# Adding gathers, and chunks prepared by VectorE's 32x32 transposes

## The chip, the cores and the metric

The kernel runs on one core of a Trainium2 chip. The metric is the device time of one execution in microseconds (us). Its engines work side by side, each on a stream of instructions in a fixed order: TensorE (PE, matmuls and transposes by matmul), VectorE (DVE), ScalarE (ACT), GpSimd (POOL), and SyncE (SP), which issues most of the DMAs. Instructions wait for each other through semaphores.

## What is computed

The input `x` is (4, 32, 128, 128) in float32. Layer 0 is an attention between channels; layer 1 reads its result as tokens of 128 values, adds a linear attention, and then a mixture of eight experts, of which each token takes the best two.

```python
# layer 0: 2x2 space to depth gives 128 "channels" of 4096 positions in each image
q = xs.reshape(B, C*R*R, hw)
energy = einsum('bci,bcj->bij', q, q)
d = sqrt(diagonal(energy))
attn = softmax(energy / (d[:, :, None] * d[:, None, :]), axis=-1)
x = gamma * einsum('bcj,bij->bci', q, attn) + xs           # and depth back to space
# layer 1: tokens t of D = 128
t = t + linear_attention(layernorm(t))                      # 8 heads
top_p, top_i = top_k(softmax(layernorm(t) @ router_w + router_b), 2)
out = t + sum_k top_p[k] * (layernorm(t) @ expert_w[top_i[k]] + expert_b[top_i[k]])
```

As the einsums have it, `energy` runs over the 4096 positions i, j and sums over the 128 channels, so it is 4096x4096 for each of the four images.

## The kernel before

**Layer 0.** The 4096 positions of an image are cut into eight chunks of 512. `attend(b)` goes through row chunks i = 0..7 and, as `energy` is symmetric, only through column blocks up to i. For each block TensorE makes `pe` (line 550) from the normalised chunk `qn`; ScalarE takes the exponential and its sum into `pr` (553); TensorE multiplies `pr` into the output `po` (439). The block's mirror image is had by transposing: VectorE turns 32x32 pieces (`F`, 368), SyncE sends them through memory (472, 487) so that the pieces change places, and TensorE multiplies them into `pg` (374), which VectorE adds to the output `o` (384). ScalarE sums them up once more (`junk`, 379).

**Preparation.** `prep(b, kc)` makes two chunks at a time ready, sixteen times in all, four for each image. SyncE loads rows `xx` with tokens on the partitions (278); TensorE transposes them eight times into `ptq` (312); VectorE copies the result to `qT` (301), squares it (323), and sums (324); GpSimd raises the sums to -1/2 (`rn`, 163); VectorE multiplies (`qs`, 337); TensorE transposes eight times more into `ptn` (345); ScalarE copies to `qn` (343). In image 0 the first preparation stands before everything, and `keep_running` gives TensorE spare transposes while it waits. The rows that layer 1 needs again (`T`) are loaded by `input_rows`.

**Layer 1.** `close_rows` (673) divides the output by its sums, adds the input (`df`, 703; `T`, 725), takes the mean and variance for the layer norm (728), with the power `rsa` on GpSimd (163), and normalises into `xn` on ScalarE (638). `matrix`, `attention_rows` and a router follow, with a second norm whose power is `rsf`. For images 0 to 2, `sorted_experts` then works in two halves of 16 groups of 128 rows: it scatters each row twice into a buffer `xs` sorted by expert (indirect DMAs from GpSimd's queue, 989), loads tiles of that buffer (1015), multiplies each by its expert (1058, 1051), copies the result (1034) and stores it in `ys`, gathers the two rows of each token from `ys` (`yb`, 1116) and adds them with their weight to `acc` on VectorE (1085), which had been fetched from memory. For image 3, whose layer 1 has no attention beside it, all eight experts are computed densely (`py`, 1200), and nothing is sorted.

**Order.** PE, DVE, ACT and SP are in an order written out by hand: instructions stand in each engine's queue as the program emits them. The main loop (1325 to 1368) runs through the steps of `attend`, and after each lets other generators go one step. Those in `timed` have a begin and an end in per cent of the image and a count of steps; those in `steady`, the layer-1 stream of the image before, go a step each ten units of a clock of 1568 units per image. GpSimd's powers and gathers are kept in their program order by `pinned`. Scatters and gathers also wait for the newest exponential (`exps`), so that no more of them run than the steps have. `hold` gives out a bank of PSUM and its eviction. The layer-1 work of image b runs beside the attention of image b+1.

Of the kernel before, what the change touches and what calls it, by code (L numbers as in the profile page):

```python
# [22 lines left out]
def kernel(  # L23
# [94 lines left out]
    NT = 2 * HR + E - 1  # L118
    rank_below = const.tile([P, P], F32, tag="below", name="rank_below")
# [5 lines left out]
    xs = [dram.tile([NT * P, D], F32, tag=f"xs{h}", name=f"xs_{h}", bufs=1) for h in range(2)]  # L125
# [9 lines left out]
    def setup_sorting():  # L135
# [14 lines left out]
        rows = x.rearrange("b c h w -> (b c h) w")  # L150
# [130 lines left out]
    def prep(b, kc, st):  # L281

        if b == 0:
            if kc == 0:
                st["all"] = big1.tile([P, 4, 8, HW2, 2], F32, tag="T", name="xx_0")
            xx = st["all"][:, kc]
        else:
            xx = xin.tile([P, 8, HW2, 2], F32, tag="xx", name=f"xx_{b}_{kc}")
        first = b == 0 and kc == 0
        load_tokens(  # L290
            xx.rearrange("p k w r -> p k (w r)"), b, 8 * kc, 8, (nc.sync, nc.scalar if first else nc.sync)
        )
# [3 lines left out]
        yield  # L296
        yield
        yield from idle(2 if b else 1)

        def load_half(g, pt):  # L300
            nc.vector.tensor_copy(
                qT[:, :, 2 * g : 2 * g + 2, :].rearrange("p s j (r c) -> p (j r) s c", c=64),
                pt.rearrange("p (m s c) -> p m s c", s=2, c=64),
            )

        for g in range(2):
            yield
            pt, done = hold(f"ptq_{b}_{kc}_{g}", partial(load_half, g))
            for jj in range(2):
                for r2 in range(2):  # L310
                    k = 4 * g + 2 * jj
                    nc.tensor.transpose(  # L312
                        pt[:, ts(2 * jj + r2, P)], xx[:, k : k + 2, :, r2].rearrange("p k w -> p (k w)"), ident
                    )
            yield
            done()
        yield
# [3 lines left out]
        for s in range(2):  # L321
            sq = work.tile([P, NJ, P], F32, tag="qs", name=f"sq_{b}_{kc}_{s}", bufs=2)
            nc.vector.tensor_tensor(sq, qT[:, s], qT[:, s], ALU.mult)
            nc.vector.tensor_reduce(ss[:, ts(s, NJ)], sq, AX.X, ALU.add)  # L324
            if first:
                pow_neg_half(rn[:, ts(s, NJ), 0], ss[:, ts(s, NJ)])
            elif s == 1:
                pow_neg_half(rn[:, :, 0], ss)
            yield
            yield  # L330
        yield from idle(1)
        if first:
            keep_running(22, ps_g, "pg")
# [5 lines left out]
        for s, qs in enumerate(scaled):  # L339
            yield  # L340
            qn = npool.tile([P, CH], F32, tag="qn", name=f"qn_{b}_{2 * kc + s}")
            st.setdefault("qn", {})[2 * kc + s] = qn
            pt, done = hold(f"ptn_{b}_{kc}_{s}", lambda p, qn=qn: nc.scalar.activation(qn, p, AF.Copy))  # L343
            for j in range(NJ):
                nc.tensor.transpose(pt[:, ts(j, P)], qs[:, j, :], ident)
            yield
            done()
        yield
        yield
# [19 lines left out]

    def transposed_share(b, st, i, jc, G):  # L370

        pg = ps_g.tile([P, CH], F32, tag="pg", name=f"pg_{b}_{i}_{jc}")
        for ib in range(NJ):
# [8 lines left out]
            if ib == NJ - 1:  # L382
                o = st["o"][jc].rearrange("p (j a c) -> p a j c", a=4, c=S)
                nc.vector.tensor_tensor(o, o, pg.rearrange("p (a j c) -> p a j c", a=4, c=S), ALU.add)  # L384
                st["got"][jc] += 1
            yield "done" if ib == NJ - 1 else None

    def diagonal_share(b, st, i, G):
# [3 lines left out]
        for step in ((3,), (2, 1)):  # L392
# [9 lines left out]
            if step == (2, 1):  # L402
                o = st["o"][i].rearrange("p (j a c) -> p a j c", a=4, c=S)[:, :, :3]
                nc.vector.tensor_tensor(
                    o, o, pg[:, : 3 * P].rearrange("p (a j c) -> p a j c", a=4, c=S), ALU.add
                )
                st["got"][i] += 1
# [8 lines left out]
    def attend(b, st):  # L416
# [11 lines left out]
        for i in range(NCH):  # L428
# [5 lines left out]
            def values(w, blk, lo, hi, i=i, row=row):  # L434
# [7 lines left out]
                if row["left"] == 0:  # L442
                    o = opool.tile([P, CH], F32, tag="o", name=f"o_{b}_{i}")
                    nc.scalar.activation(o, row["po"], AF.Copy)  # L444
                    st["o"].append(o)
# [63 lines left out]
            def back(w, j, jc, i=i):  # L509
# [7 lines left out]
                if j == NJ - 1:  # L517
                    nc.vector.tensor_tensor(st["o"][jc], st["o"][jc], row["back"], ALU.add)
# [68 lines left out]
    def input_rows(b, st):  # L587
        st["T"] = T = big1.tile([P, KT, D], F32, tag="T", name=f"T_{b}")
        nk = 4 if b == 0 else 8
        for k in range(0, KT, nk):  # L590
            load_tokens(T[:, k : k + nk, :], b, k, nk)
            yield
            yield
            yield from idle(1)

    def layer1(b, st):
# [3 lines left out]
        xn = big1.tile([P, KT, D], F32, tag="xn", name=f"xn_{b}")  # L600
# [5 lines left out]
        place = stat.tile([P, 2, KT], U32, tag="place", name=f"place_{b}", bufs=1)  # L606
# [29 lines left out]
        def normalise(rows, rs, nb):  # L636
            for k in rows:
                nc.scalar.activation(xn[:, k, :], T[:, k, :], AF.Identity, scale=rs[:, k, :], bias=nb[:, k, :])  # L638

        def transpose_rows(g):  # L640
            pt, done = hold(f"ptx_{b}_{g}", partial(keep_rows, g))
            for j in range(4):
                nc.tensor.transpose(pt[:, ts(j, P)], xn[:, 4 * g + j, :], ident)
# [15 lines left out]
        def gram_rows(rows):  # L659
# [9 lines left out]
            for k in rows:  # L669
                nc.tensor.matmul(p[:, :D], xn[:, k, :], xn[:, k, :], start=(k == rows[0]), stop=(k == rows[-1]))  # L670
            return done

        def close_rows(kc):
# [23 lines left out]
            def divide(pb):  # L697
                for s in range(2):
                    own = slice(s * 64, s * 64 + 64)
                    o = st["o"][2 * kc + s]  # L700
                    for r2 in range(2):
                        rows = slice(r2 * 64, r2 * 64 + 64)
                        nc.vector.tensor_tensor(  # L703
                            df[own, :, :, r2],
                            o[rows].rearrange("p (k w) -> p k w", w=HW2),
                            pb[own].rearrange("p (k w) -> p k w", w=HW2),
# [29 lines left out]
            if late_rows:  # L736
                for j in range(k + 4, k + 8):
                    nc.vector.tensor_scalar(
                        xn[:, j, :], T[:, j, :], rsa[:, j, :], nba[:, j, :], ALU.mult, ALU.add
# [122 lines left out]
        def transpose_tokens(g, alloc=psum_t):  # L862
# [3 lines left out]
                lambda p: nc.scalar.activation(xn[:, ts(g, 4), :], p.rearrange("p (j t) -> p j t", t=P), AF.Copy),  # L866
                alloc,
            )
            for j in range(4):
                nc.tensor.transpose(pt[:, ts(j, P)], xn[:, 4 * g + j, :], ident)  # L870
# [43 lines left out]
        def sorted_experts(h):  # L914
# [72 lines left out]
            for n in range(2 * HR):  # L987
                k, i = r0 + n // 2, n % 2
                inst = nc.gpsimd.indirect_dma_start(xs[h], offset(place[:, i, k : k + 1]), xn[:, k, :], None)  # L989
# [11 lines left out]
                if h == 1 and n in (7, 15):  # L1001
                    yield from idle(2)
# [11 lines left out]
            def load(g, n):  # L1014
                inst = nc.sync.dma_start(bufs[g % 4][:, :n], rows_of(xs[h], g, n))
# [3 lines left out]
            def products(turned, applied):  # L1019


                def leave(p):
                    if turned:
                        g, n = turned
                        nc.scalar.activation(  # L1025
                            bufs[4 + g % 2][:, :n], p[:, : n * P].rearrange("p (j t) -> p j t", t=P), AF.Copy
                        )
                    if applied:
                        g, n = applied
                        if g % 4 < 2:  # L1030
                            result = bufs[6 + g % 2]
                        else:
                            result = work.tile([P, 2, D], F32, tag="grp", name=f"result_{b}_{h}_{g}", bufs=2)
                        nc.vector.tensor_copy(  # L1034
                            result[:, :n], p[:, 2 * P : 2 * P + n * D].rearrange("p (j c) -> p j c", c=D)
# [4 lines left out]
                if applied:  # L1040
# [9 lines left out]
                    for j in range(n):  # L1050
                        nc.tensor.matmul(  # L1051
                            p[:, 2 * P + j * D : 2 * P + j * D + D], bufs[4 + g % 2][:, j, :],
                            weights[:, bass.ds(begins[2 * (g % 2) + j], D)], start=True, stop=True,
                        )
                if turned:
                    g, n = turned
                    for j in range(n):
                        nc.tensor.transpose(p[:, ts(j, P)], bufs[g % 4][:, j, :], ident)  # L1058
                return done

            done = None
# [18 lines left out]
            accs, yb = {}, {}  # L1080

            def combine(n):
                k, i = r0 + n // 2, n % 2
                a = accs[k // 4]
                nc.vector.scalar_tensor_tensor(
                    a[:, k % 4, :], yb[k // 4][:, i, k % 4, :], weight[:, i, k, :], a[:, k % 4, :], ALU.mult, ALU.add
                )
                if k % 4 == 3 and i == 1:
                    after_steps.append((now[0] + 2, partial(put, k // 4)))

            def fetch(g):
                nc.scalar.dma_start(accs[g], t2[:, ts(g, 4)])
# [7 lines left out]
            dst_out = tokens(out, b)  # L1100
            after_steps = []
            now = [0]

            def due():
                now[0] += 1
                for at, f in [q for q in after_steps if q[0] <= now[0]]:
                    f()
                after_steps[:] = [q for q in after_steps if q[0] > now[0]]

            for n in range(2 * HR):  # L1110
                k, i = r0 + n // 2, n % 2
                if k % 4 == 0 and i == 0:
                    accs[k // 4] = work.tile([P, 4, D], F32, tag="acc", name=f"acc_{b}_{k // 4}", bufs=3)
                    after_steps.append((now[0] + 1, partial(fetch, k // 4)))
                    yb[k // 4] = work.tile([P, 2, 4, D], F32, tag="wide", name=f"yb_{b}_{k // 4}")
                inst = nc.gpsimd.indirect_dma_start(  # L1116
                    yb[k // 4][:, i, k % 4, :], None, ys, offset(place[:, i, k : k + 1])
                )
                wait_for(pinned(inst).ins, exps, "not more of these at a time than steps have")
# [288 lines left out]
```

## Time and profile before

| | before |
|---|---|
| median of 3 runs, us | 1698.8 |
| lowest and highest | 1698.34, 1700.94 |
| profiled execution, us | 1704.26 |
| its span, us | 1702.5 |
| mean TensorE clock granted | 0.993 |
| HBM read, written, MB | 153.85, 175.24 |

The profiled execution has its own time, 5.5 us above the median; durations below are from it. A group's line in the profile gives the code line, the engine and its operation, the tiles written and read with their form, how often, then busy time in us with the mean of one in ns, and last the idle time of the engine just before, with what ended it. These are the groups that the change touches:

```profile
L312 PE MATMUL ptq<-ident,xx 128*128 128x128 f32 x128 | 21.0, 290 | 9.3 <-DMA xx<-in_x_dram 9.3
L345 PE MATMUL ptn<-ident,qs 128*128 128x128 f32 x128 | 20.3, 283 | 6.8 <-issue 6.1 <-DVE qs L337 0.6
L301 DVE COPY qT<-ptq 128x512 f32<-128x512 f32 x32 | 21.7, 679 | 31.8 <-PE ptq L312 25.7 <-PE pe L550 6.1
L337 DVE TENSOR_TENSOR qs<-qT,rn 128x512 f32<-128x512 f32 x32 | 20.6, 681 | 1.5 <-POOL rn L163 1.5
L1085 DVE SCALAR_TENSOR_TENSOR acc<-yb,weight,acc 128x128 f32<-128x128 f32 x192 | 65.7, 343 | 4.0 <-DMA acc<-t 0.5
L1116 POOL DMA_INDIRECT yb<-ys,place x192 | 185.3, 965 | 246.7 <-ACT pr L553 67.9 <-DMA xn<-xs 63.2 <-issue 44.0
```

Read the first: TensorE made 128 transposes of `xx` into `ptq`, the records of one lasted 290 ns on average, and TensorE stood idle for 9.3 us before some of them, until a load of `xx` had landed. Records of neighbouring matmuls overlap, so busy times on PE add up to more than the engine's time. A piece of the chain of waits has a start in us, a length, and the line of the instruction that the end of the run depended on there. A line of a wait list names who waited, for whom, and the total in us, how many times, and the longest.

### The profile page before, as it was taken

How to read it: one execution, taken by the hardware profiler on the slowest of the kernel's cores; microseconds unless marked ns; L12 is line 12 of the kernel's file. 1: busy time of each engine (PE TensorE's matmuls, PEld its weight loads, DVE VectorE, ACT ScalarE, POOL GpSimd, SP SyncE). 2: the span in 40 equal slices, each digit the busy share in tenths (PEclk: the TensorE clock that was granted, in tenths of full speed). 3: DMA queues.
4: the chain of work that ended last, by engine and by line, in shares of the span. 5: the costliest groups of instructions: out<-in, count | busy, mean ns of one | idle time of the engine just before them, and what ended most of it. 6: DMA issues, size and time to landing. Idle time of an engine off the chain costs nothing.

```text
span 1702.5 us, 21925 instructions
## 1 busy us (share of the span) xinstructions
PE 1651.5 (97%) x5458; PEld 876.1 (51%) x5458; DVE 936.7 (55%) x2443; ACT 926.0 (54%) x2893; POOL 511.0 (30%) x553
## 2 busy tenths in 40 slices
PE   8999999999999999999999999999999999998888
PEld 5444444455554555445554455545555455554643
DVE  4433334467485345478478334556748533454787
ACT  3555445466575555446565555545656455544476
POOL 1000000011026425451015642543102642446166
PEclk9999999999999999999999999999999999999999
DMA  4554756754458777875457777886445876876001
GB/s 135 168 177 157 204 173 219 242 190 162 149 173 266 229 239 243 255 225 161 136 179 235 228 248 240 236 258 194 165 141 167 264 228 216 254 243 193 7 12 39
DMA packets 227053, 325.51 MB, mean 191 GB/s; under 512 B 31472, under 2 KB 155504, under 8 KB 212592
## 3 DMA queue, kind: packets, MB, share of 16 engines
q1 hardware_dynamic: 206416, 285.15, 52.3%
q0 software_dynamic: 12288, 25.19, 5.1%
q10 hardware_dynamic: 8224, 13.77, 2.8%
q8 instruction: 46, 0.75, 0.2%
q14 instruction: 79, 0.65, 0.1%
HBM read 153.85 MB, written 175.24 MB: 193 GB/s over the span
## 4 chain that ended last, share of the span: by engine, by line
PE 79%; DVE 8%; DMA 4%; ACT 3%; issue 2%; SPq 2%; POOL 1%; another core or an unknown queue 0%; ACTq 0%; DVEq 0%; POOLq 0%
PE po L439 22%; PE pe L550 22%; PE pg L374 19%; PE pys L1051 3%; PE py L1200 3%; PE pg L395 2%; PE pys L1058 1%; PE pat L796 1%; ACT xn L638 1%; SPq L487 1%; DMA F<-blocks 1%; DVE df L703 1%; PE pgram L670 1%; PE ptq L312 1%; DMA blocks<-F 1%
## 5 line engine op out<-in xcount | busy, mean ns | idle before, releaser
L553 ACT ACTIVATE pr<-pe 128x512 f32<-128x512 f32 (+1 forms) x576 | 322.4, 560 | 552.0 <-PE pe L550 420.6
L439 PE MATMUL po<-pr,qT 128*128 128x512 f32 (+3 forms) x1152 | 551.9, 561 | 6.3 <-ACT o L444 5.6
L550 PE MATMUL pe<-qn,qn 128*128 128x512 f32 x896 | 462.5, 598 | 5.2 <-ACT pr L553 4.9
L374 PE MATMUL pg<-F,qT 128*128 128x512 f32 x880 | 451.1, 594 | 1.3 <-DMA F<-blocks 1.3
L368 DVE STREAM_TRANSPOSE F<-pr 128x512 f32<-128x512 f32 x440 | 305.8, 702 | 165.8 <-ACT pr L553 144.2
L439 PEld LDWEIGHTS po<-pr,qT 128*128 128x128 f32 x1152 | 216.0, 191 | 254.1 <-issue 223.7
L379 ACT ACTIVATE junk<-F 128x512 bf16<-128x512 f32 x440 | 272.9, 620 | 1.4 <-DMA F<-blocks 1.4
L374 PEld LDWEIGHTS pg<-F,qT 128*128 128x128 f32 x880 | 167.5, 191 | 197.2 <-issue 182.4
L1116 POOL DMA_INDIRECT yb<-ys,place x192 | 185.3, 965 | 246.7 <-ACT pr L553 67.9
L989 POOL DMA_INDIRECT xs<-xn,place x192 | 185.8, 968 | 163.0 <-ACT pr L553 86.7
L550 PEld LDWEIGHTS pe<-qn,qn 128*128 128x128 f32 x896 | 154.3, 192 | 114.7 <-issue 98.2
L384 DVE TENSOR_TENSOR o<-o,pg 128x512 f32<-128x512 f32 x110 | 75.4, 685 | 189.5 <-PE pg L374 156.2
L163 POOL TENSOR_TENSOR rn<-ss,neg_half 128x8 f32<-128x8 f32 (+1 forms) x17 | 26.9, 1584 | 332.6 <-DVE ss L324 332.5
L553 ACT ACTIVATION_READ_ACCUMULATOR pr<-pe 128x1 f32 x576 | 112.1, 195 | 0.0
L1025 ACT ACTIVATE xn<-pys 128x256 f32<-128x256 f32 x120 | 45.3, 378 | 109.8 <-PE pys L1058 87.5
L163 POOL TENSOR_TENSOR rsf<-dm_f,neg_half 128x8 f32<-128x8 f32 (+1 forms) x15 | 26.2, 1744 | 233.7 <-DVE sv_f L630 233.7
L1051 PEld LDWEIGHTS pys<-ew_sb,xn 128*128 128x128 f32 x468 | 69.6, 191 | 46.6 <-issue 43.8
L550 PE MATMUL pe<-qn 128*128 128x512 f32 (+3 forms) x256 | 90.4, 435 | 0.7 <-ACT qn L343 0.7
L379 ACT ACTIVATION_READ_ACCUMULATOR junk<-F 128x1 f32 x440 | 84.4, 192 | 0.0
L163 POOL TENSOR_TENSOR rsa<-dm_a,neg_half 128x8 f32<-128x8 f32 x16 | 26.5, 1654 | 186.5 <-DVE sv_a L630 186.2
L1034 DVE COPY xn<-pys 128x256 f32<-128x256 f32 x60 | 25.4, 424 | 89.2 <-ACT xn L1025 68.7
L1034 DVE COPY result<-pys 128x256 f32<-128x256 f32 (+1 forms) x60 | 24.6, 410 | 87.1 <-ACT xn L1025 57.8
(212 smaller groups left out, 1655.4 us busy)
## 6 DMA issues: line engine op xcount, KB each, us to landing
blocks<-F SPq DMA_DIRECT2D x110, 1024.0 KB
F<-blocks SPq DMA_DIRECT2D x220, 192.0 KB
F<-blocks SPq DMA_DIRECT2D x220, 128.0 KB
xn<-xs SPq DMA_DIRECT2D x114, 128.0 KB
F<-blocks SPq DMA_DIRECT2D x220, 64.0 KB
below<-F SPq DMA_DIRECT2D x31, 384.0 KB
out_dram<-acc SPq DMA_DIRECT2D x128, 64.0 KB
xx<-in_x_dram SPq DMA_DIRECT2D x62, 128.0 KB
```

Of the source, the lines that this page charges most:

```text
L163: pinned(nc.gpsimd.tensor_tensor(dst, src, neg_half.to_broadcast(list(src.shape)), ALU.pow))
L368: f()
L374: nc.tensor.matmul(pg.rearrange("p (a f) -> p a f", a=4), st["qT"][i][:, ib, :], G[:, :, ib], start=(ib == 0), stop=(ib == NJ - 1),)
L379: nc.scalar.activation(junk, G[:, :, ib], AF.Copy, accum_out=st["sums"][:, NJ * i + ib, jc : jc + 1])
L384: nc.vector.tensor_tensor(o, o, pg.rearrange("p (a j c) -> p a j c", a=4, c=S), ALU.add)
L439: nc.tensor.matmul(row["po"][:, lo:hi], qT[blk // NJ][:, blk % NJ, :], w, start=start, stop=(row["left"] == 0))
L550: nc.tensor.matmul(pe[:, c0:], qn[jc][:, ts(j, P)], qn[i][:, c0:], start=True, stop=True)
L553: nc.scalar.activation(pr[:, c0:], pe[:, c0:], AF.Exp, accum_out=sums[:, t, i : i + 1]).ins
L989: inst = nc.gpsimd.indirect_dma_start(xs[h], offset(place[:, i, k : k + 1]), xn[:, k, :], None)
L1051: nc.tensor.matmul(p[:, 2 * P + j * D : 2 * P + j * D + D], bufs[4 + g % 2][:, j, :], weights[:, bass.ds(begins[2 * (g % 2) + j], D)], sta ...
L1116: inst = nc.gpsimd.indirect_dma_start(yb[k // 4][:, i, k % 4, :], None, ys, offset(place[:, i, k : k + 1]))
L1200: nc.tensor.matmul(bank, xn[:, k, :], ew_sb[:, 4 * h : 4 * h + 4, :], start=True, stop=True)
```

## The change

The change has four parts.

1. *Preparation.* A chunk's transposed rows `qT` are made by VectorE. Rows are loaded by quarters (`load_quarters`, `xa`, with channels on the partitions in groups of 32), and four 32x32-block transposes write `qT` in place of eight TensorE transposes and two copies. `qn` is made from the rows `xx` (token order), which VectorE multiplies with a bank of PSUM that holds `rn` spread out: two copies (`wide`), four TensorE transposes (`pnorm`) and four products (`scale`) stand in place of two products, eight transposes and two ScalarE copies. The columns of a chunk come in another order for that, so some views of `o` and `df` change. The first preparation (`prep_first`) keeps the eight transposes into `ptn`, and has 40 spare transposes rather than 22.
2. *Loads and placement.* For image 0 the rows `T` are loaded by the preparations, and `input_rows` is used for images 1 to 3 alone. For images 1 to 3 a preparation loads both `xa` and `xx`. Preparations have 16 steps rather than 12 or 13, over longer stretches of the image.
3. *Rows with their weight.* A row of `xs` has 132 values, of which the last four repeat the row's weight; GpSimd writes them into `xn` before each half of the scatters. The result of an expert is multiplied by that weight as it leaves PSUM, so `ys` holds weighted rows. Loads have six buffers rather than four.
4. *Adding gathers.* `acc` is fetched first, and the gathers add to it in the DMA itself (`compute_op`). VectorE's 192 combines and the tile `yb` go. The second four gathers of a group add to the same rows as the first four and wait for them. Gathers come one to two generator steps (images 0 and 1), or two with a pause after each four (image 2). Scatters have more pauses.

```diff
+    def load_quarters(b, kc, queues=(nc.sync, nc.sync)):
+        xa = xin.tile([P, 2, 2, 2, HW2, 2], F32, tag="xx", name=f"xa_{b}_{kc}")
+        halves = x[b].rearrange("c (s g) w -> c s (g w)", s=2)
+        for a in (0, 2, 1, 3):
+            first_row = 16 * kc + 4 * a
+            queues[a // 2].dma_start(
+                xa[ts(a, S)].rearrange("p s k r w e -> p s (k r w e)"),
+                halves[:, :, first_row * W : (first_row + 4) * W],
+            )
+        return xa
+    def turn_quarters(s, xa, qT):
+        for k in range(2):
+            nc.vector.transpose(
+                qT[:, s, 2 * k : 2 * k + 2, :].rearrange("p h (e r c) -> p r (h e) c", e=2, r=2),
+                xa[:, s, k].rearrange("p r (h t) e -> p (r h) e t", h=2),
+            )
...
     def prep(b, kc, st):
-        for g in range(2):
-            pt, done = hold(f"ptq_{b}_{kc}_{g}", partial(load_half, g))
-            for jj in range(2):
-                for r2 in range(2):
-                    k = 4 * g + 2 * jj
-                    nc.tensor.transpose(
-                        pt[:, ts(2 * jj + r2, P)], xx[:, k : k + 2, :, r2].rearrange("p k w -> p (k w)"), ident
-                    )
+        for s in range(2):
+            turn_quarters(s, xa, qT)
+            yield
+        if b > 0:
+            xx = xin.tile([P, 8, HW2, 2], F32, tag="xx", name=f"xx_{b}_{kc}")
+            load_tokens(xx.rearrange("p k w r -> p k (w r)"), b, 8 * kc, 8)
...
+        def scale(s, spread, view):
+            qn = channels(b, kc, s, st)
+            own = slice(s * 64, s * 64 + 64)
+            for r2 in range(2):
+                nc.vector.tensor_tensor(
+                    qn[ts(r2, 64)].rearrange("p (j a t) -> p a j t", a=4, t=S),
+                    xx[own].rearrange("p (a k) (h t) r -> p r a (k h) t", a=4, h=2)[:, r2],
+                    view(spread[own]), ALU.mult,
+                )
...
+        wide = work.tile([P, NJ, 2, 64], F32, tag="qs", name=f"wide_{b}_{kc}", bufs=2)
+        for s in range(2):
+            nc.vector.tensor_copy(wide[:, :, s], rn[:, ts(s, NJ)].to_broadcast([P, NJ, 64]))
         yield
+        bank, done = hold(f"pnorm_{b}_{kc}", scale_all)
+        for j in range(NJ):
+            nc.tensor.transpose(bank[:, ts(j, P)], wide[:, j].rearrange("p s c -> p (s c)"), ident)
...
             for n in range(2 * HR):
-                k, i = r0 + n // 2, n % 2
-                inst = nc.gpsimd.indirect_dma_start(xs[h], offset(place[:, i, k : k + 1]), xn[:, k, :], None)
+                i, k = n // HR, r0 + n % HR
+                if n % HR == 0:
+                    pinned(
+                        nc.gpsimd.tensor_copy(xn[:, half, D:], weight[:, i, half, :].to_broadcast([P, HR, DW - D]))
+                    )
...
-                        nc.vector.tensor_copy(
-                            result[:, :n], p[:, 2 * P : 2 * P + n * D].rearrange("p (j c) -> p j c", c=D)
+                        result = keep["results"][:, g % 4]
+                        nc.vector.tensor_tensor(
+                            result[:, :n], p[:, 2 * P : 2 * P + n * D].rearrange("p (j c) -> p j c", c=D),
+                            bufs[g % 6][:, :n, D : D + 1].to_broadcast([P, n, D]), ALU.mult,
                         )
...
+            rate = 1 if b < B - 2 else 2
+            fetch(groups[0])
+            yield from idle(2)
+            for g in groups:
+                for n in range(8):
+                    i, k = n // 4, 4 * g + n % 4
+                    inst = nc.gpsimd.indirect_dma_start(
+                        accs[g][:, n % 4, :], None, ys, offset(place[:, i, k : k + 1]), compute_op=ALU.add
+                    )
+                    wait_for(pinned(inst).ins, exps, "not more of these at a time than steps have")
+                    if (n + 1) % rate == 0:
+                        yield
+                        yield
+                    if rate == 2 and n % 4 == 3:
+                        yield from idle(1)
+                    if n == 3 and g != groups[0]:
+                        put(g - 1)
+                    if n == 3 and g != groups[-1]:
+                        fetch(g + 1)
...
-            for kc, begin, end in ((1, 0, 5), (2, 6, 20), (3, 25, 45)):
-                timed.append((prep(0, kc, states[0]), begin, end, 12))
+            for kc, begin, end in ((2, 6, 22), (3, 25, 48)):
+                timed.append((prep(0, kc, states[0]), begin, end, 16))
...
-            timed.append((prep(b + 1, 0, nxt), 65, 82, 13))
-            timed.append((prep(b + 1, 1, nxt), 87, 99, 13))
-        begin, end, count = (52, 94, 17) if b == 0 else (36, 47, 9)
-        timed.append((input_rows(b, states[b]), begin, end, count))
+            timed.append((prep(b + 1, 0, nxt), 52, 78, 16))
+            timed.append((prep(b + 1, 1, nxt), 80, 99, 16))
+        if b > 0:
+            timed.append((input_rows(b, states[b]), 36, 47, 9))
...
-            timed.append((prep(b + 1, 2, nxt), 2, 20, 13))
-            timed.append((prep(b + 1, 3, nxt), 30, 50, 13))
+            timed.append((prep(b + 1, 2, nxt), 1, 22, 16))
+            timed.append((prep(b + 1, 3, nxt), 28, 52, 16))
```

## The prediction

> **What bounds the kernel now.** I read the page's busy times first, then the chain of waits in order of time in a quiet stretch, then TensorE's wait list, and then the chain again wherever that list had an entry.
>
> ```profile
> PE 1651.5 (97%) x5458; PEld 876.1 (51%) x5458; DVE 936.7 (55%) x2443; ACT 926.0 (54%) x2893; POOL 511.0 (30%) x553
> ...
> 642.02 0.86 PE pg L374 x2
> 642.87 0.47 PE ptq L312 x4
> 643.34 0.45 PE pys L1051 x4
> ...
> 656.97 0.86 PE pe L550 x2
> ```
>
> TensorE is busy 97% of the span, and in the quiet stretch one matmul group begins where the last ends: a group taken out of it shortens the kernel by its pace on the chain. That pace is 0.43 us for a 512-wide matmul and 0.47 us for four transposes; the group table's mean of 290 ns for one transpose has the overlap of pipelined matmuls in it and must not be multiplied.
>
> ```profile
> PE ptq L312 <- DMA xx<-in_x_dram: 9.3, 3, 5.7
> PE ptn L345 <- issue: 6.1, 2, 3.1
> PE po L439 <- ACT o L444: 5.6, 13, 2.0
> ...
> 711.96 3.12 DMA acc<-t
> ...
> 717.00 1.37 SPq L278
> 718.41 4.54 DMA xx<-in_x_dram
> ...
> 723.41 0.72 PE ptq L312 x4
> 724.13 1.52 PE pe L550 x2
> ...
> 746.47 1.36 issue
> 747.84 0.91 PE ptn L345 x4
> 748.75 1.71 PE pe L550 x2
> ```
>
> The wait list totals what TensorE lost and for whom. The two largest entries belong to the chunk preparation. In images 1 and 2 the same thing happens twice: at 711 and 1118 us SyncE stands behind a fetch of `acc`, so rows arrive late for `ptq`; at 747 and 1149 us `ptn` waits while VectorE works off a queue of combines, gated differences and transposes. After such a gap a pair of `pe` takes 1.71 us where 0.86 is usual. At the four places TensorE waits 2.06, 3.07, 1.52 and 3.07 us, and the slow matmuls after them lose 2.9, 1.9, 0.5 and 3.2 us (their pieces minus their usual pace): 18.2 us together.
>
> **The Trainium skill.** "TensorE: Matmul & The Clock Gate", Part 1, says that the clock halves after an idle window of some 3.4 us and returns after about as long at work. The trace agrees in kind, 0.86 to 1.71 us, though 3.07 us of idling were enough. "DMA: Bandwidth & Descriptors", in the part on SWDGE and HWDGE, says that adding during a transfer belongs to GpSimd's DMAs; its rules for kernel authors say that an adding DMA reads its destination and writes it later with nothing held between, so a second add to the same rows must wait for the first. The trace of before has no adding DMA. "VectorE: DVE Perf Modes", The three transpose paths, says that VectorE turns 32x32 blocks only; hence the new loads by quarters and the changed column order. Its one trace form here is `F` (L368, 702 ns for 128x512).
>
> **The change, part by part.** Sums are against the profiled execution, 1704.3 us (span 1702.5), which stands 5.5 us above the median of 1698.8; I carry the difference over to the median.
>
> *Preparation on TensorE.* A preparation of two chunks now has 8 `ptq` and 8 `ptn`; after, four transposes into one bank. Four `ptn` take 0.44 us on the chain. 2x0.47 + 2x0.44 - 0.44 = 1.38 us, times 15 preparations (the first is separate): -20.7 us, all on the bounding engine.
>
> *Preparation elsewhere.* VectorE loses two `qT` copies (679 ns) and two `qs` products (681) and gains four 128x256 transposes (0.42 us each, estimated between the 283 ns of a 128x128 and 702 of a 128x512), two 128x256 copies (367, as L694) and four 64x512 products from PSUM (687, as L703): +2.4 us each, +37 us in all. The 192 combines go: -65.7. The products of result and weight take the place of copies (424 ns) at about their price. VectorE thus falls by some 29 us from 936.7, which costs and gains nothing directly. ScalarE loses 2x0.59 us x15 = 18 us. The output evictions that become strided and the reordered gated difference I take at their old price; bounds -0.1 to +0.2 us each, some 150 of them, beside TensorE's work.
>
> *Loads.* Images 1 to 3 load each chunk pair twice, by quarters and by rows: 48 more issues of 128 KB, image 0 16 fewer 64 KB ones, so SyncE issues 32 more at 0.45 us = 14 us over 1700; 6.3 MB on 325.5. Every step is stretched over 16 stream steps rather than 13, so a load stands 5 steps (some 24 us) ahead of its transposes where it took 4.5 to 5.8 us. A SyncE wait as at 711 us then no longer reaches TensorE. If this cover went, each chunk pair would cost the 5 us of before.
>
> *First chunk.* Before: rows land at 5.5, eight `ptq` to 7.7, copies, first `pe` at 13.64. After: two transposes (0.84) in place of `ptq` and a copy (2.7), -2 us. The 40 spare matmuls at 0.19 us (22 took 4.21) make 7.6 us, need no loaded row and end by about 10, before `ptn`.
>
> *Stalls of 18.2 us.* The `ptq` ones (7.0) lose their consumer. The `ptn` ones (11.2) come from VectorE's backlog, which loses its combines but gets 2.4 us more of preparation. Bounds 0 and -18; I take -12, as `pnorm` waits only for VectorE's small copies, but its products must still be made before the chunk's turn, at i=4, 21% into the image: 19.4% is where the plan puts them, some 6 us of cover.
>
> *Adding gathers in the middle.* POOL's instruction count stays at 192 gathers and 192 scatters of 0.96 us, plus twelve small copies. In images 0 and 1 the gathers are spread one to two stream steps (5 us), 64 over 320 us where they took 160; a fourth-next gather waits for the first to land, 20 us later, hidden for any credible landing. What queues behind a waiting gather on POOL are the powers `rn`, `rsa`, `rsf`, and behind these VectorE and ScalarE's `xn`: 0 to +8 us, I take +2. Rows of 528 rather than 512 bytes in `xs`: 3% on 25 MB, nothing.
>
> *The tail.* Here POOL is on the chain.
>
> ```profile
> L1116 POOL DMA_INDIRECT yb<-ys,place x10: 943/948/1036, 1560.9 to 1572.4; - x10
> ...
> 1593.91 1.64 POOL rsa L163
> ...
> 1605.12 0.18 DVE dm_a L627
> 1605.78 1.64 POOL rsa L163
> ...
> 1607.73 0.50 ACT xn L638
> 1608.27 2.07 PE pgram L670 x16
> ```
>
> Before, ten gathers of image 2 started from 1560.9 to 1572.4, 1.26 us apart, and none stood between the `rsa` of 1593.9 and that of 1605.8. After, the slower pace leaves 20 of image 2's gathers in POOL's order between these two. From the end of the earlier one, 1595.8 less the 2.2 us of combines that leave the chain there, 20x1.26 = 25.2 us: `rsa` begins at 1619 rather than 1605.8, +13 us on the path to the end. TensorE idles over 10 us meanwhile and starts slowly: +3 us, as after the gaps above. Bounds: 0 if most of the 20 are issued earlier in POOL's idle time; and if an add takes longer to land than four issues (5.04 us), each of three second halves of a group waits the difference. I take a landing of 5 us, an estimate from the 2.75 to 3.1 us of `acc<-t` and a read of the destination besides: +16 in all.
>
> Sum: -20.7 - 2 - 12 + 2 + 16 = -16.7, so 1687.6 by the profiled execution and about 1682 against the median.
>
> **Rivals.**
> (a) *Slower than before: slow adds in the tail.* Should an add take 14 us to land, the three waits add 3x9 = 27 to the sum of -16.7: +10, so 1709. It decides from a landing of 5.04 + 16.7/3 = 10.6 us on. For it: nothing in before shows such an add, and POOL's next power stands in line behind all of them. Against it: ten plain gathers were issued back to back with semaphores reused eight apart, so a plain one lands within some 10 us.
> (b) *No tail cost.* The 20 gathers go out in gaps, or the last rows are late for other reasons: -20.7 - 2 - 12 - 2 = -37, with some stall left 1665. For it: POOL sat idle 9.96 us before the `rsa` of 1605.8. Against it: order on an engine is fixed, and their predecessors wait for exps.
> (c) *The stalls stay or move.* `qn` is now made by VectorE, with no ScalarE help; when it is late at i=4, a 3 us gap and the slow clock cost 5 us per image, and the 12 us saved are paid back: 1694. For it: 6 us of cover only, and VectorE's slices reach 8 tenths there.
> (d) *The change doesn't do what it says*: transposes leave TensorE by the instruction order; no chance given.
>
> **How the numbers follow.** Main case 1682 (1674 to 1690), 0.47; (b) 1665, 0.18; (c) 1694, 0.16; (a) 1709, 0.19, into which I put a power on POOL that is late by more than its +8 as well. Leaving out the ends of (a) and (b): 1658 to 1706. A measurement of this kernel can tell about 0.2%, 3.4 us, from no change: bounds 1695.4 and 1702.2. Main and (b) are faster, of (c) two fifths (0.06): 0.71. Of the rest of (c) 0.09 falls within and a little above: slower 0.20.
>
> **What would show it.** Right: no `ptq` and TensorE busy some 21 us less; first `pe` near 11.7; no TensorE gap over 2 us in the stretches of 700 to 760 and 1115 to 1160; VectorE near 908; the last `rsa` near 1590 with a string of gathers before it. Wrong: a gather whose semaphore wait lasts over 5 us in mid-image; `pe` waiting for `qn` at i=4; powers on POOL late behind gathers; TensorE's clock row under 9 in a middle slice.

## The result, and the profile after

The changed kernel takes 1704.2 us (median of 7 runs, 1701.5 to 1706.0) beside 1698.3 for the kernel before: a ratio of 1.0037, interval 1.0025 to 1.0048. The forecast was 1682. A repeat beside other runs (e12 below) gave 1703.2 and 1.0073 (1.006 to 1.0086). So the change makes the kernel slower by 0.4 to 0.7%; the profiled spans, 1702.4 after and 1702.5 before, hide this, because the first trace of before was an execution 5.5 us above its median. A second trace of before (e4) has a span of 1696.0; it is used for comparisons below where it is named. The kernel before took 1698 to 1700 us beside the first runs and 1690 to 1692 beside e5 to e12, so times are compared beside each other's before, and a lead read between traces of different sets of runs can be off by several us.

The page of the changed kernel first: busy times, the granted clock by slices, the software DMA queue (packets, MB, share), and the group of the gathers.

```profile
PE 1629.5 (96%) x5288; PEld 858.7 (50%) x5288; DVE 910.2 (53%) x2343; ACT 913.3 (54%) x2863; POOL 630.5 (37%) x565
...
PEclk9999999999999999999999999999999999999699
...
q0 software_dynamic: 33792, 25.58, 8.5%
...
L1162 POOL DMA_INDIRECT acc<-ys,place x192 | 301.4, 1570 | 300.1 <-ACT pr L610 171.2
```

TensorE is busy 22 us less and VectorE 26 us less, as the change meant. GpSimd is busy 120 us more, and 116 of these are in the gathers: 1570 ns each where 965 were. The software queue moves the same 25 MB in 33792 packets where it had 12288. In one slice near the end the clock is at 6 tenths.

TensorE's wait list after (who waited for whom; us in total, times, longest):

```profile
PE pgram L726 <- ACT xn L694: 34.4, 4, 29.6
PE pnorm L397 <- DVE F L419: 5.8, 3, 2.0
PE pe L607 <- ACT pr L610: 5.0, 7, 1.9
...
PE pnorm L397 <- DVE wide L388: 2.5, 1, 2.5
```

In images 1 and 2 neither the wait of before for `xx` nor that of `ptn` for VectorE is left. One wait of 29.6 us has come, and smaller ones for `pnorm`. The chain of waits, in order of time, shows where the large one ends:

```profile
1563.13 0.04 POOL rsa L164
...
1565.58 0.30 POOL acc L1162
...
1599.62 1.54 POOL acc L1162
1601.16 0.30 issue
1601.46 1.54 POOL acc L1162
1603.00 1.72 POOL rsa L164
...
1605.03 0.50 ACT xn L694
...
1605.58 3.79 PE pgram L726 x16
...
1609.74 2.73 PE pgv L837 x6
```

Between the two `rsa` stand GpSimd's adding gathers without a break. The last `rsa`, and with it `xn`, `pgram` and all that ends the kernel, waits for the last of them. Before, the same `rsa` began at 1605.78 right after its operand; now it begins at 1602.45 (the timeline's own start of it), although the attention ended 30.7 us earlier than in that trace (1566.7 against 1597.4). `pgram` takes 3.79 us where it took 2.07.

How far each kernel had come, in us: ScalarE's copy of each image's eighth row chunk to `o` (called the end of the image below), the start of the last `rsa`, and the span. "Before" is the second trace.

| | before (e4) | adds only (e6) | prep only (e5) | changed |
|---|---|---|---|---|
| image 0 | 365.1 | 366.2 | 358.9 | 358.3 |
| image 1 | 769.5 | 762.3 | 760.1 | 753.6 |
| image 2 | 1173.3 | 1160.4 | 1159.9 | 1152.0 |
| image 3 | 1592.0 | 1571.5 | 1573.4 | 1566.7 |
| last `rsa` | 1600.4 | 1607.3 | 1581.8 | 1602.5 |
| span | 1696.0 | 1707.0 | 1678.4 | 1702.4 |

By the end of the attention the changed kernel is 25.3 us ahead; at the last `rsa` it is 2.1 us behind.

### The profile page after: what moved, and what is told of

Its sections match the earlier page's. It is cut to its first block, busy times and chain, and to the rows that moved or that the text cites. A ratio compares the mean times of both kernels' runs of the same rounds, so it can differ in the third digit from the quotient of the medians.

```text
span 1702.4 us, 21468 instructions
## 1 busy us (share of the span) xinstructions
PE 1629.5 (96%) x5288; PEld 858.7 (50%) x5288; DVE 910.2 (53%) x2343; ACT 913.3 (54%) x2863; POOL 630.5 (37%) x565
## 3 DMA queue, kind: packets, MB, share of 16 engines
q0 software_dynamic: 33792, 25.58, 8.5%
## 4 chain that ended last, share of the span: by engine, by line
PE 77%; DVE 10%; DMA 4%; POOL 3%; ACT 2%; issue 2%; SPq 1%; DVEq 0%; ACTq 0%; POOLq 0%
PE po L495 22%; PE pe L607 21%; PE pg L431 19%; PE pys L1111 3%; PE py L1247 2%; POOL acc L1162 2%; PE pgram L726 2%; PE pg L451 2%; DVE F L419 2%; PE pys L1118 1%; PE pat L852 1%; DVE df L759 1%; DMA blocks<-F 1%; SPq L543 1%; DMA F<-blocks 1%
## 5 line engine op out<-in xcount | busy, mean ns | idle before, releaser
L1162 POOL DMA_INDIRECT acc<-ys,place x192 | 301.4, 1570 | 300.1 <-ACT pr L610 171.2
L1093 DVE TENSOR_TENSOR results<-pys,xn 128x256 f32<-128x256 f32 x120 | 49.8, 415 | 183.8 <-ACT xn L1087 146.3
L694 ACT ACTIVATE xn<-T,nba,rsa 128x128 f32<-128x128 f32 x120 | 49.2, 483 | 44.6 <-POOL nba L688 44.6
L726 PE MATMUL pgram<-xn 128*128 128x128 f32 x256 | 38.7, 294 | 34.7 <-ACT xn L694 34.4
L1111 PE MATMUL pys<-ew_sb,xn 128*128 x468 | 71.6, 274 | 0.0
```

The lines of the kernel that those rows point to most:

```text
L726: nc.tensor.matmul(p[:, :D], xn[:, k, :D], xn[:, k, :D], start=(k == rows[0]), stop=(k == rows[-1]))
L1093: nc.vector.tensor_tensor(result[:, :n], p[:, 2 * P : 2 * P + n * D].rearrange("p (j c) -> p j c", c=D), bufs[g % 6][:, :n, D : D + 1].to_ ...
L1111: nc.tensor.matmul(p[:, 2 * P + j * D : 2 * P + j * D + D], bufs[6 + g % 2][:, j, :D], weights[:, bass.ds(begins[2 * (g % 2) + j], D)], st ...
L1162: inst = nc.gpsimd.indirect_dma_start(accs[g][:, n % 4, :], None, ys, offset(place[:, i, k : k + 1]), compute_op=ALU.add)
```

## The experiments

**e4: before again.** No edit.

> The kernel before itself, for a second trace. If TensorE's four stalls beside the preparation of images 1 and 2 (18 us in the first trace) belong to the kernel, they are there again, of the same length; if they belong to that one execution, which was 5.5 us above the median, some are missing and the span is near 1697.

The ratio to before was 1.0012 (0.9997 to 1.0028). The span was 1696.0 and the stalls were all there:

```profile
PE ptq L312 <- DMA xx<-in_x_dram: 10.9, 3, 5.7
PE ptn L345 <- issue: 6.1, 2, 3.1
```

They belong to the kernel (5.7 of the first line is the start). At the four places the timeline has 2.62, 3.07, 2.51 and 3.07 us, against 2.06, 3.07, 1.52 and 3.07 in the first trace. The difference between the two traces lies elsewhere, some 3 us of it in image 3 (from the end of image 2 to that of image 3 it is 418.7 us here, 421.7 in the first trace), and was not traced further.

**e5 and e6: each half alone.** e5 has the new preparation, loads, column order and placement, with plain gathers and VectorE's combines; e6 has the rows with their weight and the adding gathers, with the old preparation.

> The kernel before with the new preparation, loads, column order and placement alone; gathers plain, combined on VectorE, in the old order. TensorE's removed transposes (20.7) and the first chunk (2) give 22.7; the stalls of before give 0 to 12 more: 1664 to 1676 by theory A, in which the preparation is good and the gathers lose it. If the preparation itself gains little (its VectorE work turns up in waits), 1685 to 1698.

> The kernel before with rows that carry their weight and adding gathers alone; preparation as before. Theory A: 20 gathers at 1.84 us stand between the last two rsa: 36.9 us from 1593.6, so the last rsa begins near 1630 in place of 1605.8, +25, and +3 for the clock; less what stalls go with the combines (0 to 11): 1715 to 1727. If adding gathers cost nothing on the path to the end, 1687 to 1698.

e5: 1677.4 beside 1692.4, ratio 0.9909 (0.9892 to 0.9926). e6: 1708.4, ratio 1.0095 (1.0078 to 1.0111). So the adding gathers alone make the kernel slower and the preparation alone makes it faster. e6's list shows both halves of its effect:

```profile
PE pgram L671 <- ACT xn L639: 30.8, 5, 29.6
PE ptq L313 <- DMA xx<-in_x_dram: 5.8, 1, 5.8
```

The last wait is as long as in the changed kernel, and of the stalls of images 1 and 2 none is left (5.8 is the start). The table says the same: without one transpose removed, e6 is 20.5 us ahead of before at the end of image 3, and 6.9 behind at the last `rsa`. With that lead e6 stayed below the 1715 to 1727 expected, in which at most 11 us were allowed for stalls. The table also shows that the two halves do not add up: 20.5 and 18.6 us by the end of image 3 give 25.3 together. The timed runs don't add up either: -15.0 us for e5 and +16.0 for e6 make +1.0, and the whole change measured +5.9 and +12.9.

e5 gained less than the 22.7 us expected. In its list of TensorE's waits one entry has grown, from 0.8 us in e4 (1.6 in the changed kernel):

```profile
PE pg L430 <- DMA F<-blocks: 5.1, 3, 2.6
```

Two of these waits, 2.59 and 1.90 us, are at 716 and 1116 us, near the places where rows came late before. Whether the same delay of SyncE's transfers reaches another consumer there was not traced.

**e10: before without its combines.**

```diff
-                nc.vector.scalar_tensor_tensor(
-                    a[:, k % 4, :], yb[k // 4][:, i, k % 4, :], weight[:, i, k, :], a[:, k % 4, :], ALU.mult, ALU.add
-                )
```

> The kernel before with VectorE's 192 combines left out, so that the experts' part is missing from the output; gathers, stores and all else stay. If the combines are what fills VectorE when ptn waits, and their lateness what holds up SyncE's stores ahead of the xx loads, the four stalls of images 1 and 2 go and the time falls by 14 to 20 us plus some 2 in the tail: 1677 to 1683. If the gathers' DMAs or the fetches of acc cause them, the ptq stalls stay and the time falls by under 10.

1682.5 beside 1692.0, 9.5 us less, ratio 0.9951 (0.9938 to 0.9965). Timeline of TensorE, pieces that follow a gap in the stretches of the four stalls:

```profile
722.97 0.72 PE L312 MATMUL ptq<-ident,xx 128*128 128x128 f32 x4 [2.69 <-DMA xx<-in_x_dram]
...
1121.59 1.10 PE L312 MATMUL ptq<-ident,xx 128*128 128x128 f32 x4 [2.83 <-DMA xx<-in_x_dram]
```

The two waits of `ptn` are gone and the two of `ptq` are not: the combines filled VectorE ahead of `ptn`, but they are not what delays the `xx` loads. In e6, which has the loads and transposes of before, these waits are gone as well, so it is the new gather part's fetches, stores or pace that relieves them; which of these was not separated.

**e2: the same gathers, without the addition.**

```diff
-                        accs[g][:, n % 4, :], None, ys, offset(place[:, i, k : k + 1]), compute_op=ALU.add
+                        accs[g][:, n % 4, :], None, ys, offset(place[:, i, k : k + 1])
```

> The changed kernel with the gathers' addition left out (the rows of acc are overwritten, so neither the fetched rows nor the first expert's are in the output); order and waits as in the changed kernel. Theory A1 (it is GpSimd's own time for an adding gather that is longer, 1.84 us from one to the next where a plain one takes 1.26): spacing 1.26, last rsa 20 x 0.58 = 11.6 us earlier, about 1692 (1689 to 1695). Theory A2 (an indirect DMA into rows that others wait for is as slow without the addition): 1.84 stays, 1704.

1684.3 beside 1699.9 where about 1692 was expected, ratio 0.9915 (0.9895 to 0.9936). The same tile's gathers in the last 100 us, in the changed kernel and then in e2 (least, median and most ns; first and last start):

```profile
L1162 POOL DMA_INDIRECT acc<-ys,place x28: 1537/1539/2637, 1540.5 to 1601.5; - x28
```

```profile
L1162 POOL DMA_INDIRECT acc<-ys,place x26: 943/947/1728, 1539.4 to 1583.2; - x26
```

With the addition, GpSimd is held 1539 ns by each, without it 947; the 0.30 us between two are the same. From the end of image 3 to the last `rsa` the changed kernel has 35.8 us and e2 23.7: 12.1 less for 20 gathers, where 11.6 were expected. A further 6.3 us are there already at the end of image 3, so the longer gathers cost time in the middle too: the two waits of `pgram` at 786 and 1185 us of the changed kernel are 1.3 us each in e2, 2.1 there. The software queue is back at 12288 packets. It is GpSimd's own time to issue an adding gather, then, not a wait for landing: in the changed kernel's series the pause between two is 0.30 us throughout, also where the second half of a group follows the first, and the list of POOL's waits has 0.3 us in all for earlier adds. Nor does a crowded queue explain it: the 89 adding gathers between 1100 and 1540 us, many of them after a pause, took 1532 ns at least and 1547 in the median.

**e7: the order in the tail.** The gathers left at the end are put around the last powers: 6 before the last `rsa`, 6 after it, 8 behind the second `rsf`.

```diff
             stats_of(1)
+            feed(9)
...
                 close_stats("f", 16, 16, bs)
+                feed(40)
...
-    for steps, _ in steady:
-        for _ in steps:
+    def feed(n):
+        until = gathers[0] + n
+        while gathers[0] < until and next(steady[2][0], "end") != "end":
             pass
-    closing.last_parts()
+
+    feed(4)
+    for _ in steady[3][0]:
+        pass
+    feed(6)
+    closing.last_parts(feed)
```

`feed(n)` issues gathers until `n` more have gone out, or none is left.

> The changed kernel, with the adding gathers that are left at the end put around the last powers instead of all ahead of them: 6 stand between the last two rsa (20 in the changed kernel), 6 between the last rsa and the first rsf, 8 behind the second rsf. Nothing else moves. If POOL's order in the tail is the whole loss: last rsa near 1575 in place of 1602.5, no slow clock after it, the ratio to before near 1.0037 - 0.018 = 0.985 (about 1674 beside 1699). If the gathers behind the rsa then hold up something else (rsf, a store, acc), half of it comes back: 0.993.

1680.5 beside 1692.0, ratio 0.9937 (0.9916 to 0.9957); the changed kernel's repeat had 1703.2 beside 1690.3. The attention ends at 1567.2, as in the changed kernel (1566.7), and the chain goes on:

```profile
1576.16 1.54 POOL acc L1162
1577.70 1.71 POOL rsa L164
1579.73 0.50 ACT xn L694
1580.28 3.69 PE pgram L726 x16
1584.34 2.10 PE pgv L837 x6
```

The last `rsa` begins 25.3 us earlier, and the span is 23.1 us shorter (1679.3; 20.9 against the span of e12, 1700.2). So 14 of the 20 gathers, moved away from in front of one power, are worth 21 to 23 us, of which the forecast had reckoned with most: its sum delays that power by 15.4. The gain is not the 30 us of e7's first theory; the ratio is that of its second, 0.993. The last `rsf` began at 1624.5, 47.3 us after the last `rsa`, where before (e4) has 40.1 and the changed kernel, with its slow start, 43.2. The gathers that were moved behind the second `rsf` held up GpSimd's sums of the dense experts (`tmp`, the first at 1615.74, right behind the last gather), and behind these stood the last `rsf`.

**e1: gathers of image 2 sooner.**

```diff
-                    if rate == 2 and n % 4 == 3:
-                        yield from idle(1)
```

> The changed kernel without the pause after each four adding gathers of image 2; nothing else. Theory A (the loss is POOL's order in the tail: 20 gathers at 1.84 us stand ahead of the last rsa): the instruction order leaves 2 gathers between the last two rsa, which fit into POOL's idle time there; the last rsa begins near 1575 in place of 1602.5, the clock after it stays full: about 1704.2 - 27.5 - 3 = 1674 (1669 to 1679). Theory B (the gain in the middle is small, and adding gathers cost time all along): 1695 to 1704.

1692.9 beside 1699.9, ratio 0.9958 (0.9942 to 0.9974): 11 us below the changed kernel where 30 were expected. The list has, in place of one wait of 29.6 us,

```profile
PE pgram L726 <- ACT xn L694: 16.4, 8, 5.1
```

The last `rsa` begins at 1589.3, but the end of image 3 went from 1566.7 to 1580.3: the gathers came out from before the last power and stood before the earlier ones, for which `pgram` waited 4.46, 1.24 and 5.08 us. From 1516.9 to 1576.7 us GpSimd issues a gather every 1.84 us, with only two powers between. What is short is GpSimd's time in these last 60 us or so, not in the whole of image 3: between 1350 and 1450 us it is busy for a third.

**e3: TensorE kept busy through most of the wait.** `keep_running(36)` became `keep_running(280)`.

> The changed kernel with 280 spare transposes in place of 36 ahead of the last sum of products, which fill TensorE's 29.6 us of waiting (0.115 us each, 32 us in all). If the halved clock after that wait costs what the trace shows (products 3.79 in place of 2.07 us, the next group 2.73 in place of 2.10), the time falls by 2 to 3 us: 1701.5. If the clock has no part, 1704.

1705.4 beside 1699.9, ratio 1.0033 (1.0022 to 1.0044): not to be told from 1.0037. The trace shows why this settles little: the spare transposes ended at 1602.8, a gap of 3.0 us was left, and `pgram` ran slowly after it all the same:

```profile
1605.76 3.57 PE pgram L726 x16
1609.79 2.07 PE pgv L837 x6
```

`pgv` is back at 2.07 us, `pgram` is not (it takes 3.69 in e7 too, after a wait of 3.8 us). By the durations, the slow start of the changed kernel costs 1.7 us in `pgram` and 0.6 in `pgv`. The span of e3 is 1.7 us shorter, and the timed runs show no gain; what a wait without any gap would bring was not measured.

**e8: the copies for `pnorm` one step earlier**, on top of e7.

```diff
-        for _ in range(ahead - 2):
+        for _ in range(ahead - 3):
             yield
         wide = work.tile([P, NJ, 2, 64], F32, tag="qs", name=f"wide_{b}_{kc}", bufs=2)
...
         yield
+        if ahead > 2:
+            yield
```

> As e7_tail_order, and in each preparation the two copies that pnorm waits for are made one generator step earlier, with one more step between them and pnorm. In the trace of the changed kernel TensorE waits 1.9 to 2.5 us for them in each of the four images and its clock halves after it. If that is what keeps the removed transposes from paying, the waits go and the time falls by another 6 to 10 us against e7_tail_order; if VectorE is simply too full there, a wait of the same length comes at the products that follow, and the time is the same.

1676.0 beside 1692.0, ratio 0.9911 (0.9892 to 0.9931), 4.5 us below e7. The chain of the changed kernel at one of the places:

```profile
505.46 0.30 DVE runs L990
...
506.73 0.63 DVE F L419
507.37 0.42 issue
507.79 0.66 PE pnorm L397 x4
...
508.89 1.49 PE pe L607 x2
510.37 1.71 PE po L495 x2
```

VectorE works off the sorting's `runs` and an `F`; only then come the two `wide` copies, and TensorE stands for 1.91 us. What follows runs slowly: `po` 1.71 us for a pair where 0.86 is usual, and the granted clock over the next 5 us is 0.66. In e8 the timeline of TensorE has at this place

```profile
506.39 0.60 PE L399 MATMUL pnorm<-ident,wide 128*128 128x128 f32 x4
507.80 0.39 PE L1001 MATMUL pcnt<-runs,rank_below 128*128 128x8 f32 x2 [0.80 <-DVE runs L992]
...
508.99 1.02 PE L497 MATMUL po<-pr,qT 128*128 128x512 f32 x2
```

`pnorm` no longer waits; a gap of 0.8 us, for `runs`, is left behind it, and the pair of `po` is at its usual 1.02 (busy time, with overlap). By the end of image 3 e8 is at 1561.4 where e7 is at 1567.2, a little less than the 6 to 10 us expected.

**e9 and e11: plain gathers for image 2 alone.** e9 is the changed kernel with plain gathers into `yb` and an addition on VectorE for image 2, at the pace of before; e11 adds e8's earlier copies.

```diff
+            if b == B - 2:
...
+                    inst = nc.gpsimd.indirect_dma_start(
+                        yb[k // 4][:, i, k % 4, :], None, ys, offset(place[:, i, k : k + 1])
+                    )
```

> The changed kernel with plain gathers and VectorE additions for image 2 alone, at the pace of the kernel before; images 0 and 1 keep adding gathers. No gather stands between the last two rsa. Expected: the tail's loss goes (-30), VectorE's 64 additions cost a few us beside the attention of image 3: 1674 to 1681 beside 1699. If plain gathers at the old pace hold up the rsa of image 3, over 1685.

> e9_plain_image2 and the earlier copies of e8_tail_wide together: TensorE's three waits of 1.9 us for pnorm go, as they did in e8 (5.8 us in the span between e7 and e8). 1672.8 - 5.8 = a span of 1667, a ratio to before of 0.987. If VectorE, which has 64 additions more in image 3, gets late elsewhere, 0.991.

e9: 1676.6 beside 1692.0, ratio 0.9919 (0.9898 to 0.9940). e11: 1671.0 beside 1690.3, ratio 0.9878 (0.9863 to 0.9893). The last `rsa` of e11 begins at 1574.15, 9.2 us after the end of image 3. Its span is 2.3 us below e9's, not 5.8. e11 is faster than both kernels, by 1.2% than before and by 32 us than the changed one.

**e12: the changed kernel again**, beside e11.

> The changed kernel again, beside e11 on the same chip. If the tail is as in its first trace, 20 gathers 1.84 us apart ahead of the last rsa and a ratio to before of 1.003 to 1.005; the difference to e7_tail_order would then be what the order in the tail costs, 23 us by the spans.

1703.2, ratio 1.0073 (1.006 to 1.0086); 28 gathers in the tail with a median of 1539 ns, a wait of `pgram` of 29.6 us, and the last `rsa` at 1602.0, as in the first trace. The ratio is above the 1.003 to 1.005 expected: the kernel before was 8 us faster here than beside the first runs, the changed one 1 us. Why only one of them changed stays open.

## Why the prediction was wrong

*The step that failed: the price of a gather in the tail.* The prediction put 20 of image 2's gathers between the last two `rsa`, and that was so. It priced them at 20 x 1.26 us, from the plain gathers of before, and left POOL's time per gather at 0.96 us; it looked for the risk of the addition in its landing alone. Measured were 36.9 us for the 20, 1.84 us each: +11.7 us, which e2 takes away again (12.1). The plain gather's time was used for an operation that the trace of before did not show, with no bound on it. Together with the next point it turned a gain of 17 us into a loss: the last `rsa` was 25.3 us late by e7, which keeps 6 of the 20 ahead of it, where the prediction's own sum makes it 15.4 (1619 against 1605.8 less 2.2). Its sign for being right, a last `rsa` near 1590, failed: it began at 1602.5. Between the spans of e4 and the changed kernel the forecast of -16.7 is missed by 23 us: 12 of these are here (from the end of image 3 to the last `rsa` e4 has 8.4 us and the changed kernel 35.8, 27.4 more where 15.4 were forecast), 10 in the second term, and 1 after the last `rsa`.

*The second term: stalls and removed transposes were added up.* The steps up to the end of the attention sum to -34.9 us (-20.7 - 2 - 12 + 2, and 2.2 of combines); 25.3 were measured against the second trace of before. (Against the first trace, which the prediction was worked out from, it is 30.7.) The four places had been read as 18.2 us; by the pieces of the chain the slow matmuls lose 2.0 us at the first, not 2.9, and 0.25 at the third, not 0.5, so it is 17.0, and the 12 taken stands. These stalls went entirely. But new waits came: 8.3 us for `pnorm`, of which 2.5 in the first rows of image 0, and two of 2.1 us of `pgram` for `xn`, where GpSimd's `rsa` stands behind a gather; and after two of the three waits of 1.9 us TensorE ran slowly for another 1.9 us or so. This is rival (c), in a small form: it named the products behind `pnorm` as what would be late, and the wait was for the copies ahead of it, of which the prediction said that they were all that `pnorm` waits for. e8 moved them, and 5.8 us came back at the end of image 3. The price of the gathers is in this term as well, by the 6.3 us of e2; how the rest of the shortfall divides was not separated.

*The rivals.* (a) had the sign right and the mechanism wrong: adds were waited for 0.3 us in all. In e12's trace the semaphore updates tell when the last 20 landed, 3.2 to 4.1 us after their start, well under its 10.6. Its text, that POOL's next power stands in line behind all of the gathers, is what decided, by issue time. (b) was wrong: the gathers did not go out in POOL's idle time. e1 shows that issuing them sooner moves the wait, because GpSimd has no 37 us to spare in the last 60.

*What was right.* The first `pe` of the first chunk at 11.79 us (11.7 forecast), TensorE's busy time down by 22 us (21), VectorE at 910 us (908), no wait for `xx` and no gap over 2 us in the two stretches named, and the range for powers late in mid-image (4.3 us of waits, within 0 to 8). The clock after the long wait was put at 3 us; the durations of `pgram` and `pgv` give 2.35.

## What to carry to other kernels

An operation that moves work from a half-idle engine to another is to be priced on the engine that issues it, and a variant that the profile doesn't show gets a bound on its issue time as well as on its latency. Then the engine's queue is read at the end of the kernel, where nothing hides behind a matmul any more: here 20 issues in front of one small power cost more than all removed transposes brought. Two savings that relieve the same stall are not added; run each alone.

## What the hardware showed

An indirect gather of 128 rows of 512 bytes that adds in the DMA held GpSimd for 1.54 us and made 112 packets more than the plain one, which took 0.95 us ((33792 - 12288)/192 packets). In e12's trace, 186 adding gathers have a full record of their landing: 3.15 to 8.06 us after their start, 4.5 in the median, and 3.2 to 4.1 for the last 20, issued 1.84 us apart. With four issues between two adds to the same rows, 7.4 us, the second did not have to wait there.

A gap of TensorE of 1.91 us was enough, at 507 us in the changed kernel, for the granted clock to be 0.66 over the next 5 us and a pair of matmuls to take twice its time. But it was not always enough: after 1.98 us at 1305 us in the same trace, and after 2.69 us at 723 us in e10, the clock was 1.00 and the matmuls kept their pace. So the length of a gap alone did not decide here what followed it. The two places in the changed kernel's timeline, where 1.02 is usual for a pair of `po`:

```profile
507.79 0.66 PE L397 MATMUL pnorm<-ident,wide 128*128 128x128 f32 x4 [1.91 <-DVE F L419]
...
510.17 1.91 PE L495 MATMUL po<-pr,qT 128*128 128x512 f32 x2
...
1304.84 0.66 PE L397 MATMUL pnorm<-ident,wide 128*128 128x128 f32 x4 [1.98 <-DVE F L419]
...
1306.43 1.02 PE L495 MATMUL po<-pr,qT 128*128 128x512 f32 x2
```
